# Two cross-attention layers on one core: the second layer's value products regrouped, VectorE's order written out beside them, sums of weights taken later

## The chip, the core and the metric

The kernel runs on one core of a Trainium2 chip. The core has a matrix engine (TensorE, PE in the profile, with its weight loads as PEld), a vector engine (VectorE, DVE), a scalar engine (ScalarE, ACT), a general engine (GpSimd, POOL), a sync engine that issues transfers (SyncE, SP) and 16 DMA engines. The metric is the device time of one execution in microseconds (us); lower is better. All arithmetic is in 32-bit floats.

## What is computed

For 8 batches, two layers one after the other. `x` holds 100 rows of 1024 for a batch, the context `ctx` 1444 rows of 512. Cut to what matters:

```
# layer 0
Q, K, V = x @ Wq + bq,  ctx @ Wk + bk,  ctx @ Wv + bv
x  = x + softmax(Q K^T / 32, over the context) V @ Wo + bo
# layer 1
q, k, v = x @ Wq + bq,  ctx @ Wk + bk,  ctx @ Wv + bv
w  = softmax(q k^T / 32, over the 100 QUERIES)
x  = layernorm(w v + x) * gamma + beta
```

In layer 1 the softmax runs over the queries, so the weights of one query do not add up to 1: their sum, times `bv`, has to be added to that query's row. That is why "sums of weights" appear below.

## The kernel before

The products of weight matrices are made first, so that the context is only multiplied by small matrices: scores are `(x Wq Wk^T) ctx^T`, and values are `(w ctx) Wv`. Large products use a scheme of seven half products in place of eight (`seven_products`, L172): each operand is cut in four, sums of the quarters are formed, and seven products go into banks of PSUM, which VectorE then adds to the result.

Layer 1 goes through the batches in a loop of blocks (L864). One block (`alternated`, L805) interleaves on TensorE 48 steps `A` (batch b's weights times its context rows, L513) with 44 steps `s` (scores of batch b+2, L542). When the scores of b+2 are complete, ScalarE copies them out (L554), VectorE transposes them in 16 instructions (L589), finds maxima (L656), ScalarE takes exponentials (L658), VectorE inverts the sums and multiplies (L661, L662), and GpSimd adds up the weights over the context (`weight_sums`, L675 to L680). Batches 6 and 7 have no batch b+2 ahead of them, so their blocks hold `A` steps alone. In the block of batch 5 two `s` steps go with each `A` step (`doubled`), so that batch 7's scores are early.

The values are the second part: `A` times `Wv` (512 by 1024). They are made in three sets: batches 0 to 4 by seven half products after block 5 (`project1_halves`, moving operands of 250 columns), batches 5 and 6 by 8 plain products after block 6 (`project1`, 200 columns), and batch 7 at the very end (`project_last`, L784). VectorE adds each result to `xT`, which holds the transposed queries (L612, L722).

A batch whose values are in is finished (`finish`, L770) by: 8 transposes on TensorE (L741), then on VectorE two additions of the bias times the sums of weights (L745), statistics (L751, L756, L758) and a scaling (L760); GpSimd takes the inverse root (L759), ScalarE scales (L762), GpSimd adds beta (L763) and issues the store (L764). Batch 7, the last, has its scaling and beta on VectorE in two halves (L767), each with its store (L768), the first from SP, the second from ACT. The table `finished` (L862) says at which step of which block a batch's transposes begin: batches 0, 1, 2 in block 6, batches 3 and 4 around `project1`, batches 5 and 6 in block 7. `weight_totals` (L682) turns the sums of weights of two batches by TensorE; it comes at step 8 of blocks 1, 3, 5 and 7.

TensorE's instructions stay in the order in which they are written. The other engines are ordered by a scheduler, which also chooses buffers. PSUM has two pools: six banks for scores, value products and transposes, two for `A` and for one pair of the seven products.

## Time and profile before

| | us |
|---|---|
| median of 4 runs (lowest, highest) | 642.47 (641.96, 642.88) |
| the profiled execution | 643.34 |
| its span on the core | 641.6 |
| TensorE busy | 631.2 (98%) |
| VectorE busy | 449.8 (70%) |
| ScalarE busy, GpSimd busy | 132.2, 101.7 |

The span is cut into lines by engine, and "busy" counts the time in which at least one instruction runs. Because matmuls are pipelined, the busy time of TensorE says that it never stands without work, not that it works at its peak; how long a matmul really holds the engine is read from the distance between the starts of two neighbours. A 32-bit product is recorded as two passes, so one `matmul` of the code is two records; a transpose is one. Layer 1's blocks fill the last 200 us of the span.

### The profile page before, as it was taken

The page shows a single profiled execution, that of the slowest core. Times are in us where ns is not written, and L with a number is a line of the kernel's source. Part 1 is how long each engine was busy: PE and PEld are TensorE (multiplying, and loading weights), DVE is VectorE, ACT ScalarE, POOL GpSimd, SP SyncE. Part 2 cuts the span into 40 slices and gives each one's busy share as a digit, 9 for nine tenths or more (in the row PEclk, how much of TensorE's full clock was granted, in tenths as well). Part 3 has the DMA queues.
Part 4 walks back from the last instruction along what each step waited for, and adds up shares of the span by engine and source line. Part 5 has one row for each costly group of instructions (what it writes and reads, how often), then busy time and mean ns, then how long its engine had stood idle before and what let it go on. Part 6 is the DMA issues. An engine that isn't in the chain of part 4 may idle for free.

```text
span 641.6 us, 9823 instructions
## 1 busy us (share of the span) xinstructions
PE 631.2 (98%) x3920; PEld 517.9 (81%) x3920; DVE 449.8 (70%) x848; ACT 132.2 (21%) x337; POOL 101.7 (16%) x121
## 2 busy tenths in 40 slices
PE   8999999999999999999999999999999999999994
PEld 7886445568885999999998655556999999999992
DVE  4999959669723775666655698238777655896994
ACT  1010010100103333212330000123433244330221
POOL 5000000009200000000010000007211222112773
PEclk9999999999999999999999999999999999999998
DMA  9928018000079799988996303046789999940122
GB/s 293 379 91 329 0 51 337 0 1 0 2 280 359 257 321 303 318 305 313 312 335 219 108 1 131 1 170 209 280 296 313 305 318 311 310 172 1 52 78 77
DMA packets 47961, 127.28 MB, mean 198 GB/s; under 512 B 3944, under 2 KB 6504, under 8 KB 47916
## 3 DMA queue, kind: packets, MB, share of 16 engines
q1 hardware_dynamic: 45454, 119.63, 53.8%
q0 software_dynamic: 2064, 6.56, 3.2%
q8 instruction: 31, 0.51, 0.3%
q10 hardware_dynamic: 398, 0.47, 0.2%
q14 instruction: 14, 0.11, 0.1%
HBM read 123.36 MB, written 3.28 MB: 197 GB/s over the span
## 4 chain that ended last, share of the span: by engine, by line
PE 81%; DVE 5%; issue 5%; POOL 5%; ACT 2%; DMA 1%; POOLq 0%; SPq 0%; DVEq 0%; ACTq 0%
PE s L542 23%; PE A L513 20%; PE qk_x L141 5%; PE g_x L141 5%; PE qk_y L141 4%; PE g_y L141 3%; PE vo_x L141 3%; DVE w L589 3%; PE o_x L141 3%; POOL z L763 2%; PE qk_w L141 2%; PE vo_y L141 2%; PE o_y L141 2%; PE g_w L141 2%; PE g_z L141 2%
## 5 line engine op out<-in xcount | busy, mean ns | idle before, releaser
L513 PE MATMUL A<-w,c 120*128 120x100 f32 (+1 forms) x1536 | 245.9, 265 | 0.0
L513 PEld LDWEIGHTS A<-w,c 120*128 120x128 f32 (+1 forms) x1536 | 215.5, 190 | 0.8
L589 DVE STREAM_TRANSPOSE w<-prob 32x384 f32<-32x384 f32 (+1 forms) x256 | 143.7, 561 | 46.3 <-ACT prob L554 15.8
L542 PE MATMUL s<-cT,g0T 128*100 128x131 f32 (+2 forms) x592 | 122.7, 296 | 0.0
L542 PE MATMUL s<-cT,g1T 128*100 128x131 f32 (+2 forms) x592 | 119.3, 296 | 0.0
L542 PEld LDWEIGHTS s<-cT,g0T 128*100 128x100 f32 x592 | 78.3, 167 | 8.3
L542 PEld LDWEIGHTS s<-cT,g1T 128*100 128x100 f32 x592 | 77.5, 167 | 8.9 <-ACT g1T L418 0.9
L554 ACT ACTIVATE prob<-s,c 100x393 f32<-100x393 f32 (+2 forms) x64 | 35.1, 559 | 116.9 <-PE s L542 116.6
L658 ACT ACTIVATE w<-w,negmax 120x100 f32<-120x100 f32 (+1 forms) x96 | 34.8, 364 | 75.1 <-DVE negmax L656 75.1
L469 POOL TENSOR_SCALAR xT<-xT,L_xattn_bo 128x800 f32<-128x800 f32 x8 | 20.8, 2607 | 134.0 <-PE qk_x L141 134.0
L571 DVE TENSOR_REDUCE maxima<-prob 100x1 f32<-100x394 f32 (+3 forms) x32 | 16.6, 528 | 28.1 <-ACT prob L554 27.9
L141 PE MATMUL qk_x<-qk 128*128 128x256 f32 x128 | 29.6, 389 | 0.9 <-DMA qk<-in_L_xattn_WkT 0.9
L141 PEld LDWEIGHTS qk_x<-qk 128*128 128x128 f32 x128 | 24.5, 196 | 5.2 <-DMA qk<-in_L_xattn_WqT 1.3
L850 POOL DMA_DIRECT2D vectors<-in_L_xattn_gamma x1 | 0.6, 602 | 163.2 <-DMA c<-in_ctx 163.2
L675 POOL TENSOR_TENSOR part<-w 120x500 f32<-120x500 f32 x8 | 10.0, 1250 | 103.5 <-PE s L542 47.3
L302 DVE SCALAR_TENSOR_TENSOR qk_L_xattn_bk<-qk,L_xattn_bk,qk_L_xattn_bk 128x1024 f32<-128x1024 f32 x14 | 17.9, 1277 | 3.9 <-DMA qk<-in_L_xattn_WqT 3.9
L612 DVE TENSOR_TENSOR xT<-xT,o_x 128x400 f32<-128x400 f32 (+1 forms) x24 | 13.5, 601 | 7.9 <-PE o_x L141 7.8
L418 ACT ACTIVATE g1T<-g_x,k 128x400 f32<-128x400 f32 x6 | 3.6, 594 | 74.2 <-PE g_x L141 63.8
L658 ACT ACTIVATION_READ_ACCUMULATOR w<-w,negmax 120x1 f32 (+1 forms) x96 | 17.9, 187 | 0.0
L763 POOL TENSOR_TENSOR z<-z,vectors 100x1024 f32<-100x1024 f32 x7 | 16.5, 2356 | 8.3 <-ACT z L762 8.3
L762 ACT ACTIVATE z<-z,rstd 100x1024 f32<-100x1024 f32 x7 | 8.0, 1149 | 39.7 <-POOL rstd L759 39.6
L662 DVE TENSOR_TENSOR w<-w,rtotal 120x400 f32<-120x400 f32 (+1 forms) x24 | 15.2, 634 | 0.5
(216 smaller groups left out, 872.1 us busy)
## 6 DMA issues: line engine op xcount, KB each, us to landing
cT<-in_ctxT SPq DMA_DIRECT2D x64, 722.0 KB, 6.7
c<-in_ctx SPq DMA_DIRECT2D x48, 768.0 KB, 7.4
c<-in_ctx SPq DMA_DIRECT2D x16, 512.0 KB, 6.5
vo<-in_L_xattn_Wo SPq DMA_DIRECT2D x8, 512.0 KB, 7.0
qk<-in_L_xattn_WqT SPq DMA_DIRECT2D x8, 512.0 KB
qk<-in_L_xattn_WqT SPq DMA_DIRECT2D x15, 256.0 KB, 5.3
qk<-in_L_xattn_WkT SPq DMA_DIRECT2D x15, 256.0 KB, 6.8
c<-in_ctx SPq DMA_DIRECT2D x16, 224.0 KB, 5.8
```

Of the source, the lines that this page charges most:

```text
L141: nc.tensor.matmul(banks[n // per][:, n % per * width : (n % per + 1) * width], lhs[i][:, n * P : (n + 1) * P], rhs[i], start=(fresh and i ...
L302: nc.vector.scalar_tensor_tensor(acc, src, cols[v][:, h : h + 1], acc, ALU.mult, ALU.add)
L469: nc.gpsimd.tensor_scalar(xT[:, e, :], xT[:, e, :], out_bias[:, e : e + 1], None, ALU.add)
L513: nc.tensor.matmul(ps[:, k * T : (k + 1) * T], c[m // CQ][:r, m % CQ, k * P : (k + 1) * P], w[:r, m, :], start=(m == 0 and k == 0), stop=( ...
L542: nc.tensor.matmul(banks[n // per][:T, cuts[n] - o : cuts[n + 1] - o], q[:, k, t0 : t0 + T], cT[k][:, cuts[n] : cuts[n + 1]], start=(k == ...
L554: nc.scalar.activation(p[:, part], ps[:T, : part.stop - part.start], AF.Identity, bias=key_bias[layer][:T, b : b + 1], scale=SCALE,)
L571: nc.vector.tensor_reduce(maxima[:, n : n + 1], p[:, part], AX.X, ALU.max)
L589: nc.vector.transpose(blocks(w, r, m0 * T + q * QD, T, MC - m0), blocks(p, q, m0 * MR + r * QD, MR, MC - m0),)
L612: nc.vector.tensor_tensor(to, to, ps[:, : n * width].rearrange("p (n t) -> p n t", n=n), ALU.add)
L658: nc.scalar.activation(w[:r, m0 + m, :], w[:r, m0 + m, :], AF.Exp, bias=negmax[:r, m : m + 1], accum_out=total[:r, m : m + 1])
L662: nc.vector.tensor_tensor(w[:r, grp, :], w[:r, grp, :], rtotal[:r].unsqueeze(2).to_broadcast([r, GM, T]), ALU.mult)
L763: nc.gpsimd.tensor_tensor(z, z, beta[:T], ALU.add)
```

## The change

The sets of batches become 0 to 3, 4 to 6, and 7. Both of the first two are made by seven half products, of 200 and 150 moving columns, after block 3 and after block 6; the plain products are gone. All sums of right operands are formed ahead of the products, in a buffer of their own. Two `s` steps per `A` step in block 5 are gone. The batches' finishing is spread over blocks 4, 5 and 7.

While a value product runs, VectorE keeps the order of the program (`Vector.in_order`), and the order is written by hand: the softmax of batch 5 (none of whose VectorE steps is taken before) and of batch 7 (of which 17 steps are taken) is drawn out step by step between the additions (`room`). In all softmaxes of layer 1 the three groups' maxima now come ahead of the three groups' inversions. The addition of the fourth half product goes ahead of the next one's in all seven-product stages that only add. The sums of weights are turned at step 27 in place of 8 (still 8 in block 7). The last batch's two stores change queues. The core of the diff:

```diff
+SETS = (range(0, 4), range(4, 7), range(7, 8))
+LATER = {(1, 5): 0, (1, 7): 17}
...
+                ins = getattr(nc.vector, op)(*args, **kw)
+                return tc.keep_in_program_order(ins) if self.in_order else ins
...
         W = pair("w", bank2)
         product(W, A22, T_[3], True)
+        if put is add:
+            add(1, 0, W)
         yield
...
-        softmax(s, parts)
+        s["softmax"] = softmax(s, parts)
+        for _ in islice(s["softmax"], LATER.get((layer, b))):
+            pass
...
-    def project1_halves(A, S, At):
-        n = G1 * T // 2
...
-        T_ = ([t1[:, i * n : (i + 1) * n] for i in range(2)], Bs[0], Bs[2], Bs[1])
...
-    def project1(b0, n, A, between):
-        for e in range(EC):
-            ps = bank(f"o1_{b0}_{e}")
-            for k in range(LC):
-                nc.tensor.matmul(...)
+    def project1(bs, A, S, At, between, room):
+        n, t0 = len(bs) * T // 2, bs[0] * T
...
+        T_ = [[sums[:, (2 * k + i) * n : (2 * k + i + 1) * n] for i in range(2)] for k in range(4)]
...
+        vector.in_order = True
+        right_sums(Bs, T_)
+        for _, steps in zip_longest(seven_products(f"o1_{t0}", A, Bs, S, T_, 4, n, add, add), room, fillvalue=0):
+            for _ in range(steps):
+                next(between)
+        run(between)
+        vector.in_order = False
...
-        for half, queue in ((slice(0, E // 2), nc.sync), (slice(E // 2, E), nc.scalar)):
+        for half, queue in ((slice(0, E // 2), nc.scalar), (slice(E // 2, E), nc.sync)):
...
-            for _ in range(2 if doubled else 1):
-                next(ahead, None)
+            next(ahead, None)
...
-    finished = {(B - 2, 0): 0, (B - 2, 14): 1, (B - 2, 28): 2, (B - 1, 6): G1, (B - 1, 22): G1 + 1}
+    finished = {(4, 2): 0, (4, 16): 1, (4, 30): 2, (5, 30): 3, (7, 2): 4, (7, 15): 5, (7, 28): 6}
...
+                if b % 2 and n == (8 if b == B - 1 else 27):
+                    weight_totals(batches[b - 1 : b + 1])
...
+            between, room = {3: (batches[5], (0, 3, 3, 3, 3)), 6: (batches[7], (1, 0, 1, 1))}[b]
+            project1(bs, *AS, t, between["softmax"], room)
```

## The prediction

> **What bounds the kernel now.** I read the busy table first, then TensorE's waits, then TensorE's timeline of the last 100 us, then VectorE and GpSimd beside it. From the page: the busy table, and the shares of the chain that ended last.

> ```profile
> PE 631.2 (98%) x3920; PEld 517.9 (81%) x3920; DVE 449.8 (70%) x848; ACT 132.2 (21%) x337; POOL 101.7 (16%) x121
> ...
> PE 81%; DVE 5%; issue 5%; POOL 5%; ACT 2%; DMA 1%; POOLq 0%; SPq 0%; DVEq 0%; ACTq 0%
> ```

> TensorE is busy for all of the span but its first 2 and last 8 us. Busy alone could hide waits, so its list of waits comes next (total, times, longest, in us):

> ```profile
> PE warm L90 <- DVE mhalf L105: 1.1, 1, 1.1
> PE qk_x L141 <- DMA qk<-in_L_xattn_WkT: 0.9, 1, 0.9
> PE qk_y L141 <- DVE qk_s L152: 0.2, 1, 0.2
> ```

> Three waits, all at the start. So in layer 1 the time is the length of TensorE's queue, plus the tail behind its last product. The change can win in two ways only, a shorter queue or a shorter tail, and it loses where an engine comes too late for TensorE. TensorE's timeline of the value stage (start, length, line, operation, count; a length runs to the modelled end of the last pass, so I use distances of starts):

> ```profile
> 563.85 3.56 PE L141 MATMUL o_x<-A1T,wv 128*128 128x250 f32 x16
> ...
> 587.49 0.36 PE L513 MATMUL A<-w,c 120*128 120x100 f32 x2
> ...
> 597.64 2.82 PE L513 MATMUL A<-w,c 120*128 120x100 f32 x24
> 600.29 1.04 PE L741 MATMUL z<-ident,xT 128*100 128x128 f32 x8
> 601.36 5.68 PE L718 MATMUL o<-A1T,wv 128*128 128x200 f32 x32
> 606.87 1.04 PE L741 MATMUL z<-ident,xT 128*100 128x128 f32 x8
> 607.75 5.58 PE L718 MATMUL o<-A1T,wv 128*128 128x200 f32 x32
> 613.16 1.70 PE L513 MATMUL A<-w,c 120*128 120x100 f32 x14
> ```

> The seven half products run without a gap from 563.85 to 587.49, 23.64 us for 112 passes: 0.2111 us a pass of 250 columns. The plain ones take 5.41 us for 32 passes from 607.75: 0.1691 us a pass of 200 columns, the same 0.84 ns a column. [...]

> **TensorE's queue, part by part.**
> 1. Value products. Before: 23.64 + 5.51 + 5.41 = 34.56 us. After: 112 passes of 200 columns, 112 x 0.1691 = 18.94, and 112 of 150 columns. No row has 150 columns with full weights. The bounds are the `A` pass, 0.1104, and the 200-column pass, 0.1691; 150 x 0.00084 = 0.127 lies above what weights need, so I take 0.1271: 14.23. Together 33.17: **-1.39** (-3.3 to +3.3 by the bounds).
> 2. Block 5. An `A` with two `s` repeats every 0.651 us (543.73 to 544.38 in the timeline), an `A` with one `s` every 0.4255 (33 pairs from 528.36 to 542.40), an `A` alone takes 0.2208. Before: 22 x 0.651 + 26 x 0.2208 = 20.06. After: 44 x 0.4255 + 4 x 0.2208 = 19.60. **-0.46.**
> 3. Transposes for finishing. 64 in both, the last 8 at the same place. Between `A` steps one adds 0.31 - 0.2208 = 0.089 us; two groups of 8 stood alone (1.07 and 0.88 us; the first holds a wait of 0.2 for `A1T`, which goes with the plain products). Before: 40 x 0.089 + 1.95 = 5.51. After, 32 stand behind an `s` and ahead of an `A`, which no row shows: from 0.089 (between `A`) to 0.134 (the slow group). I take 0.110, from the group without a wait: 32 x 0.110 + 24 x 0.089 = 5.66. **+0.15** (-0.5 to +0.9).

> The turned sums of weights are as many as before; moving them from step 8 to 27 costs TensorE nothing, since `wsum` is older there. The queue's sum is **-1.70 us**.

> **Does another engine come late?** I walked the changed kernel's order on each engine with these durations: additions to `xT` 0.57 us at 400 elements and 0.67 at 500 (so 0.45 at 300), sums of right operands 0.41 at 250 (0.35 at 200, 0.30 at 150), 0.585 a transpose, 0.56 a maximum, 0.57 to 0.66 a softmax product.
> - First set, t = 0 at its first product. Batch 3's copy lands at 0.8, the eight sums end at 3.5. The first two additions end at 4.6, three transposes at 6.3, the next additions at 7.4 and 9.3, three transposes at 11.1, the additions that free the first pair's banks for its last use at 12.2. TensorE wants those banks at 5 x 2.71 = 13.5: 1.3 us of cover, if all adds take 0.57. The remaining steps end at about 24; batch 5's weights are due after block 4, at 41.
> - Second set: the 16 transposes of batch 7 fill block 6 (10.6 us against 9.4); sums end at 3.1, the same banks are free near 9.2 and wanted at 10.2: 1 us of cover. Batch 7's weights are done at 10, due at 14.2.
> - Transfers: blocks 4 and 5 become longer or equal, and the pause between blocks 3 and 4 lets loads run ahead. The change adds no wait for a transfer.
> - The layer 0 stages and the other softmaxes only swap neighbours on VectorE; nearest wait there is zero, and I take zero.

> Where this cover is gone, the wait is the overrun itself, up to about 1 us a set.

> **The tail** is where the change gives back. Block 7 now finishes three batches (steps 2, 15, 28) instead of two (6, 22). VectorE's and GpSimd's timelines show what happens when they crowd:

> ```profile
> 592.13 1.27 DVE L760 SCALAR_TENSOR_TENSOR z<-z,mv,vectors 100x1024 f32<-100x1024 f32 x1
> ...
> 606.23 3.35 DVE L760 SCALAR_TENSOR_TENSOR z<-z,mv,vectors 100x1024 f32<-100x1024 f32 x1
> ...
> 624.05 1.78 DVE L760 SCALAR_TENSOR_TENSOR z<-z,mv,vectors 100x1024 f32<-100x1024 f32 x1
> ```

> ```profile
> 606.14 2.36 POOL L763 TENSOR_TENSOR z<-z,vectors 100x1024 f32<-100x1024 f32 x1 [1.26 <-ACT z L762]
> ...
> 622.39 2.35 POOL L763 TENSOR_TENSOR z<-z,vectors 100x1024 f32<-100x1024 f32 x1 [1.26 <-ACT z L762]
> ...
> 634.85 1.52 POOL L759 TENSOR_TENSOR rstd<-rstd,mhalf 100x1 f32<-100x1 f32 x1 [4.09 <-DVE rstd L758]
> ```

> L760 alone takes 1.27 us. At 606.23 it starts under a running L763 and ends at 609.58, 1.08 after L763 does: it stood still until L763 was over. Now the walk, t = 0 at the last batch's product (626.35 before). Batch 6's transposes begin 5.1 us ahead of the last 8, 1.2 later than before (6.3). Each finish costs VectorE about 4.5 us, and starts come 3.6 us apart, so batch 5's L760 ends near -1.2, its L763 runs from 0.9 to 3.3; batch 6's L760, due at 1.3, stands until 3.3 and ends at 4.5; then L759 0.6, L762 1.15, and batch 6's L763 from 6.3 to 8.7. The last batch's L760 is due at 634.68 - 626.35 = 8.3 and stands until 8.7: **+0.35** (0, if batch 6 runs 0.4 earlier, to +2.4, a whole L763).

> [...]

> **The stores.** The first half is issued from SP at 637.19 (0.31 long), its packets run from 637.97 to 639.39; the second from ACT at 637.86 (0.57), packets from 639.01 to 640.20. SP needs 0.78 us from issue to first packet, ACT 1.15. With the queues swapped the later half comes from SP: **-0.2** (0 to -0.37; both halves then share the DMA engines).

> **Sum:** -1.70 + 0.35 - 0.2 = **-1.55 us**. On the profiled execution's 643.34 that is 641.8; the median of the runs is 642.47, 0.87 below it, so I forecast 640.9.

> **Rivals.**
> - The fixed order holds TensorE: the cover of 1.3 and 1 us in the two sets is my estimate, from additions extrapolated to new widths. For it: VectorE has about 21.5 us of work beside 18.9 us of products in the first set. Against: only two products reuse banks. Overrun 0.5 us a set: 640.9 + 1.0 = 641.9.
> - The tail takes a whole L763, +2.4 instead of +0.35, since batch 6 slips by half a microsecond or more: 643.0. Against: GpSimd stood idle for 4.09 us ahead of the last L759 before.
> - Slower: the collisions chain. L763 of batch 4 ends only 0.4 us ahead of batch 5's L760; past that, L760 of batch 5 stands too (2.08 us, as at 606.23), everything behind it slips, and the last batch pays L763 (2.36) and the store's issue (0.6) on top: tail +3 to +3.5 against -1.9 elsewhere, 643.6 to 644.1, decided once batch 6's L763 ends later than 10.2 us after the last product's start. I put it at 643.9.
> - It does not do what it says: if a 150-column pass took over 0.152 us, all gain would be gone (645.5 at 0.1691). The 131-column `s` passes, near 0.114, speak against it.

> **Numbers.** Forecast (640.2 to 641.2) 0.60; fixed order 0.15; one whole collision 0.14; chain or slow passes 0.11. The smallest change that a measurement of this kernel tells from none is about 0.2%, 1.3 us: below 641.2 is faster, above 643.75 slower. So faster 0.60, same 0.29, slower 0.11. The range runs from 640.1 (no tail cost, stores at -0.37) to 643.0 (the whole collision).

> **What would show it.** Right: `o` passes of 0.169 and 0.127 us; no wait of TensorE in layer 1; block 5 near 19.6 us plus 8 transposes; L763 of batch 6 touching the last L760; the last store from SP. Wrong: gaps in the two value stages, or more than 15.5 us from the last product's start to the span's end (15.2 now).

## The result, and the profile after

The change made the kernel slower by 0.75 us: median 643.01 of 42 runs against 642.26 of 60 runs of the kernel before, ratio 1.0011 (95% interval 1.0007 to 1.0016). The forecast was 640.9. The profiled execution took 643.13, its span is 641.4. That this is no more than before's 643.34 misleads: before's profiled execution began 0.83 us late by chance. Its first `qk_y` product starts at 20.86 us, in the changed kernel at 20.03, and nothing ahead of it was changed. So from here on I measure from that product: to the first product of the last batch (`ol`), and from there to the span's end, which the traces give to 0.01 us (641.57 before, 641.36 after).

| from the profiled executions, us | before | after | predicted |
|---|---|---|---|
| `qk_y` to `ol` | 605.49 | 605.88 (+0.39) | -1.70 |
| `ol` to the span's end | 15.22 | 15.44 (+0.23) | +0.15 |

The sum of +0.39 and +0.23, +0.62 us, agrees with the medians (0.75, interval 0.45 to 1.03). The busy table and the chain's shares of the changed kernel:

```profile
PE 629.4 (98%) x3968; PEld 518.0 (81%) x3968; DVE 456.5 (71%) x864; ACT 131.9 (21%) x337; POOL 101.5 (16%) x121
...
PE 86%; DVE 6%; POOL 2%; issue 2%; ACT 2%; DMA 1%; POOLq 0%; DVEq 0%; SPq 0%; ACTq 0%
```

TensorE is busy 1.8 us less than before (631.2), and the time is longer all the same: the queue did become shorter, and TensorE now waits. Its list of waits (total, times, longest) has two lines that before had not:

```profile
PE o_y L156 <- DVE o_t L93: 1.1, 1, 1.1
...
PE z L759 <- DVE r L715: 0.5, 1, 0.5
```

**Wait 1, in the second set.** The timeline of all engines around it (start, length, engine, line, operation; idle time ahead and what ended it in brackets). L93 is the line of a helper through which much of VectorE's work goes: tell its operations by tile.

```profile
586.28 9.45 DVE L93 STREAM_TRANSPOSE w<-prob 32x384 f32<-32x384 f32 x16
...
595.76 1.52 DVE L93 TENSOR_REDUCE negmax<-w 120x4 f32<-120x400 f32 x3
...
596.43 0.38 ACT L682 ACTIVATE w<-w,negmax 120x100 f32<-120x100 f32 x1 [7.84 <-DVE negmax L93]
...
598.47 2.20 PE L156 MATMUL o_z<-A1T,wv 128*128 128x150 f32 x16
...
600.42 0.36 ACT L682 ACTIVATE w<-w,negmax 124x100 f32<-124x100 f32 x1
...
600.78 0.47 ACT L542 COPY A1T<-A 128x400 f32<-128x400 f32 x1
601.28 0.54 DVE L93 TENSOR_TENSOR o_t<-A1T 128x150 f32<-128x150 f32 x2 [4.00 <-ACT A1T L542]
...
601.74 2.28 PE L156 MATMUL o_y<-o_t,wv_s 128*128 128x150 f32 x16 [1.06 <-DVE o_t L93]
```

Read it from below. `o_y` waits for the first sum `o_t`; VectorE stood idle for 4.00 us ahead of that sum and was released by the copy L542 of batch 6's weighted features; and this copy, whose source was complete when TensorE went on to `o_x` at 596.41, started at 600.78, because in ScalarE's queue batch 7's twelve exponentials stand ahead of it, one every 0.36 us. The exponentials are late since VectorE's 16 transposes for them fill all of block 6. By starts the wait costs more than the 1.06 us of the list, which counts from a modelled end: `o_y` starts 3.27 us after `o_z` and the next product 2.12 after `o_y`, where the pace is 2.04, 1.3 us in all.

**Wait 2, in block 5.** The same view of an earlier stretch:

```profile
576.21 0.38 PE L713 MATMUL wsum_ps<-ident,wsum 124*100 124x124 f32 x2
...
577.88 0.18 DVE L93 RECIPROCAL rtotal<-total 120x4 f32<-120x4 f32 x1 [0.73 <-ACT w L682]
...
579.33 0.18 DVE L93 RECIPROCAL rtotal<-total 120x4 f32<-120x4 f32 x1 [0.66 <-ACT w L682]
...
579.54 0.58 DVE L93 TENSOR_TENSOR w<-w,rtotal 120x400 f32<-120x400 f32 x1
...
580.04 0.41 DVE L715 TENSOR_REDUCE r<-wsum_ps 100x2 f32<-100x248 f32 x1
...
580.50 0.32 PE L759 MATMUL z<-ident,xT 128*100 128x128 f32 x1 [0.49 <-DVE r L715]
```

The sums of weights of batches 4 and 5, now turned at step 27, hold a bank of PSUM (the memory that products are written to) from 576.21 until VectorE has read them (L715). VectorE comes to that only behind two of batch 6's softmax products, which wait for exponentials, and the transposes of batch 3's finish want the bank. VectorE stood idle for 0.73 and 0.66 us meanwhile: what held the sums was its order, not its load. By starts this wait costs 0.72 us: the transpose comes 0.66 late, the next one 0.06 more.

**The tail**, GpSimd and VectorE (L781 is GpSimd's addition of beta, L778 the scaling, L782 a store's issue, L777 the inverse root):

```profile
626.86 2.34 POOL L781 TENSOR_TENSOR z<-z,vectors 100x1024 f32<-100x1024 f32 x1 [1.84 <-ACT z L780]
...
627.15 3.13 DVE L778 SCALAR_TENSOR_TENSOR z<-z,mv,vectors 100x1024 f32<-100x1024 f32 x1
...
631.97 2.35 POOL L781 TENSOR_TENSOR z<-z,vectors 100x1024 f32<-100x1024 f32 x1 [1.26 <-ACT z L780]
...
634.24 1.27 DVE L778 SCALAR_TENSOR_TENSOR z<-z,mv,vectors 100x1024 f32<-100x1024 f32 x1
```

Batch 6's scaling stood under a running addition for 3.13 us, as foreseen; the last batch's did not (1.27). It starts 8.33 us after `ol`, the same as before, and VectorE's last instruction ends 11.47 after it (before 11.48). The 0.23 us are lost behind that, in the stores.

### The profile page after: what moved, and what is told of

It is laid out like the page before. It is cut to its first block, busy times and chain, and to the rows that moved or that the text cites. A ratio compares the mean times of both kernels' runs of the same rounds, so it can differ in the third digit from the quotient of the medians.

```text
span 641.4 us, 9939 instructions
## 1 busy us (share of the span) xinstructions
PE 629.4 (98%) x3968; PEld 518.0 (81%) x3968; DVE 456.5 (71%) x864; ACT 131.9 (21%) x337; POOL 101.5 (16%) x121
## 4 chain that ended last, share of the span: by engine, by line
PE 86%; DVE 6%; POOL 2%; issue 2%; ACT 2%; DMA 1%; POOLq 0%; DVEq 0%; SPq 0%; ACTq 0%
PE s L560 23%; PE A L531 20%; PE qk_x L156 6%; PE g_x L156 5%; PE qk_y L156 4%; PE o_x L156 4%; PE g_y L156 3%; PE vo_x L156 3%; DVE w L93 3%; PE o_y L156 3%; PE qk_w L156 2%; PE vo_y L156 2%; PE qk_z L156 2%; PE g_w L156 2%; PE g_z L156 2%
## 5 line engine op out<-in xcount | busy, mean ns | idle before, releaser
L93 DVE STREAM_TRANSPOSE w<-prob 32x384 f32<-32x384 f32 (+1 forms) x256 | 143.7, 561 | 37.3 <-ACT prob L572 15.1
L560 PE MATMUL s<-cT,g1T 128*100 128x131 f32 (+2 forms) x592 | 122.9, 297 | 0.0
L93 DVE TENSOR_TENSOR xT<-xT,o_x 128x400 f32<-128x400 f32 (+1 forms) x32 | 15.9, 540 | 3.5 <-PE o_x L156 3.2
L781 POOL TENSOR_TENSOR z<-z,vectors 100x1024 f32<-100x1024 f32 x7 | 16.5, 2354 | 8.1 <-ACT z L780 8.1
L759 PE MATMUL z<-ident,xT 128*100 128x128 f32 x64 | 16.4, 274 | 0.5 <-DVE r L715 0.5
L93 DVE TENSOR_TENSOR w<-w,rtotal 120x400 f32<-120x400 f32 (+1 forms) x24 | 15.6, 650 | 0.7
```

The source lines that it names most:

```text
L93: ins = getattr(nc.vector, op)(*args, **kw)
L560: nc.tensor.matmul(banks[n // per][:T, cuts[n] - o : cuts[n + 1] - o], q[:, k, t0 : t0 + T], cT[k][:, cuts[n] : cuts[n + 1]], start=(k == ...
L759: nc.tensor.transpose(ps[:T, e * P : (e + 1) * P], xT[:, 4 * j + e, b * T : (b + 1) * T], ident)
L781: nc.gpsimd.tensor_tensor(z, z, beta[:T], ALU.add)
```

## The experiments

Theory: the regrouping did shorten the queue by about 1.7 us, and two waits, one in each of block 5 and the second set, and the stores took it back. Rivals: VectorE's fixed order holds TensorE, so that another wait comes up wherever one is removed; or the regrouping brings nothing. The table has all kernels; ratios are to the kernel before, run on the same chip beside each group of kernels (its median there was 642.05 to 642.51, so medians of different groups are compared with care). Kernels with the same code behind `ol` differ by up to 0.11 us in the last column, which is its scatter.

| kernel | median (runs) | ratio, 95% | `qk_y` to `ol` | `ol` to end |
|---|---|---|---|---|
| before | 642.26 (60) | | 605.49 | 15.22 |
| after | 643.01 (42) | 1.0011 (1.0007-1.0016) | 605.88 | 15.44 |
| e1 sums of weights early | 644.46 (7) | 1.0032 (1.0020-1.0043) | 607.88 | 15.49 |
| e2 copy on VectorE | 641.82 (11) | 0.9993 (0.9984-1.0002) | 604.58 | 15.46 |
| e3 stores back | 642.81 (11) | 1.0006 (0.9998-1.0015) | 605.89 | 15.42 |
| e4 the three together | 640.98 (11) | 0.9980 (0.9971-0.9989) | 603.86 | 15.41 |
| e5 e4, free order | 640.78 (8) | 0.9976 (0.9966-0.9986) | 603.86 | 15.43 |
| e6 exponentials later | 641.36 (11) | 0.9984 (0.9975-0.9993) | 604.58 | 15.45 |
| e7 copy three times | 644.21 (10) | 1.0027 (1.0017-1.0037) | 608.61 | 15.44 |
| e8 e4, finishes earlier | 640.73 (11) | 0.9975 (0.9966-0.9983) | 603.86 | 15.37 |
| e9 before, stores swapped | 642.20 (11) | 1.0003 (0.9994-1.0011) | 605.49 | 15.24 |
| e10 copy twice | 643.53 (11) | 1.0016 (1.0007-1.0025) | 606.44 | 15.47 |
| e11 copy five times | 646.42 (5) | 1.0061 (1.0048-1.0075) | 609.54 | 15.38 |
| e12 e5, tail in halves | 640.79 (11) | 0.9979 (0.9971-0.9988) | 603.86 | 15.35 |
| e13 e4 without batch 6's store | 640.64 (11) | 0.9978 (0.9969-0.9987) | 603.86 | 15.18 |
| e14 e4, finishes on VectorE | 640.75 (11) | 0.9979 (0.9970-0.9987) | 603.86 | 15.27 |

### The two waits

**e1** turns the sums of weights of batches 4 and 5 at step 8 again (those of blocks 1 and 3 too, on which no wait hung), which is to take wait 2 away.

```diff
-                if b % 2 and n == (8 if b == B - 1 else 27):
+                if b % 2 and n == 8:
```

> The changed kernel, but the sums of weights of batches 4 and 5 are turned and summed at step 8 of block 5, as before, instead of step 27. Theory (two new waits of TensorE and the stores eat the gain of the queue): the wait of the z transposes for r in block 5 goes, TensorE's queue is 0.5 to 0.66 us shorter from block 4 to the last product, time 643.0 - 0.6 = 642.4. Rival (VectorE is simply too full around block 5, and some other bank is late as well): the wait returns at another instruction, 643.0.

Measured 644.46, 1.45 us slower than the changed kernel; neither theory nor rival foresaw that. The wait for `r` went, and the second set starts 0.73 us earlier (575.65 us after `qk_y` instead of 576.38). But the copy that `o_y` waits for hangs on VectorE and ScalarE, not on TensorE, and came not earlier but 0.33 us later; the wait of `o_y` grew to 2.11 us. And then something new. The value products' timeline, and the busy time by stretch (stretch, its length, busy time and count of each engine; the number after POOL's brackets is TensorE's granted clock):

```profile
597.35 2.20 PE L156 MATMUL o_z<-A1T,wv 128*128 128x150 f32 x16
601.67 3.56 PE L156 MATMUL o_y<-o_t,wv_s 128*128 128x150 f32 x16 [2.11 <-DVE o_t L93]
605.03 2.64 PE L156 MATMUL o_x<-o_t,wv_s 128*128 128x150 f32 x16
607.50 2.21 PE L156 MATMUL o_w<-o_t,wv 128*128 128x150 f32 x16
```

```profile
602.00:603.00 1.00, 1.00 (x8) 1.00 (x7) 1.00 (x5) 0.00 (x0) 0.00 (x0) 0.74 0.00 0
603.00:604.00 1.00, 1.00 (x5) 1.00 (x5) 0.97 (x5) 0.00 (x0) 0.00 (x0) 0.50 0.00 0
...
605.00:606.00 1.00, 1.00 (x6) 1.00 (x6) 1.00 (x4) 0.00 (x0) 0.00 (x0) 0.55 0.00 0
606.00:607.00 1.00, 1.00 (x10) 1.00 (x10) 0.72 (x3) 0.00 (x0) 0.00 (x0) 1.00 0.00 0
```

`o_y`'s 16 passes take 3.36 us from start to next start instead of 2.04: behind the wait the clock stood at 0.50, five passes in a microsecond instead of ten. From `o_y` to `ol` it is 25.84 us here and 24.17 in the changed kernel: 1.67 us lost to the clock, which no theory had.

**e2** lets VectorE make batch 6's copy, which is to take wait 1 away.

```diff
-                    if name.startswith("A1"):
+                    if name.startswith("A1") and name != "A1_6":
                         nc.scalar.copy(dst, src)
                     else:
                         nc.vector.tensor_copy(dst, src)
```

> The changed kernel, but batch 6's weighted features (A1T) are copied from the bank by VectorE, behind batch 7's maxima, instead of by ScalarE behind batch 7's twelve exponentials. Theory: the first sums of right operands of the second set start near 598 instead of 601.3, the 1.06 us wait of o_y goes, the queue is 1.2 us shorter, time 643.0 - 1.2 = 641.8. Rival (the fixed order of VectorE is what holds TensorE, the copy is only the first to show it): a wait of 0.5 us or more comes up at a later product of that set, time 642.5 or more.

Measured 641.82, queue 1.30 us shorter. VectorE's and TensorE's rows, with the copy on VectorE:

```profile
597.50 0.56 DVE L544 COPY A1T<-A 128x400 f32<-128x400 f32 x1
...
598.17 0.54 DVE L93 TENSOR_TENSOR o_t<-A1T 128x150 f32<-128x150 f32 x2
...
600.80 2.21 PE L156 MATMUL o_y<-o_t,wv_s 128*128 128x150 f32 x16
```

The sum starts at 598.17, 2.6 us ahead of `o_y`, which follows `o_z` (598.76) at the products' own pace of 2.04 us. No other wait comes up in the set. This speaks for the theory and against the fixed order as the cause.

**e6** removes the same wait by another way: batch 7's maxima and exponentials move behind the copy in ScalarE's queue, the copy stays where it was.

```diff
-LATER = {(1, 5): 0, (1, 7): 17}
+LATER = {(1, 5): 0, (1, 7): 16}
...
-            between, room = {3: (batches[5], (0, 3, 3, 3, 3)), 6: (batches[7], (1, 0, 1, 1))}[b]
+            between, room = {3: (batches[5], (0, 3, 3, 3, 3)), 6: (batches[7], (1, 1, 0, 1, 1))}[b]
```

> The changed kernel, but batch 7's maxima and exponentials are issued inside the second set, behind batch 6's copy in ScalarE's queue, instead of ahead of it; the copy stays on ScalarE. Theory (the queue order of ScalarE made the wait of 1.06 us): the first sum starts by 598, no wait of o_y for o_t, the queue 1.2 us shorter, time 641.8 as with the copy on VectorE. Rival (the second set has too little room for batch 7's softmax): a wait of 0.5 us or more at a later product of the set or at block 7's first product, 642.3 or more.

Measured 641.36 and a queue of 604.58 us, to the hundredth that of e2. The copy runs at 596.39, the first sum at 596.92, and the exponentials between 600 and 605 are early enough. So what counted was the order in ScalarE's queue, not the engine of the copy.

**e4** puts the three edits together.

> The three edits together: sums of weights at step 8, batch 6's copy by VectorE, the stores' queues of before. Theory (the three causes are apart and add): 643.0 - 0.6 - 1.2 - 0.27 = 640.9, some 1.4 us less than the kernel before, no wait of TensorE in layer 1. Rival (fixed order or regrouping brings nothing): 642 or more, with waits of TensorE in the value stages.

Measured 640.98, 1.4 us below before (642.35 on the same chip). Its list of waits has only the one at the very start:

```profile
PE warm L105 <- DVE mhalf L120: 1.1, 1, 1.1
```

Its queue is 603.86 us: 0.72 less than e2's, so with wait 1 out of the way wait 2 is worth 0.72; 2.02 less than after's, and 1.63 less than before's. The regrouping does bring what it was said to.

**e5** leaves VectorE's order in the value stages to the scheduler, on top of e4.

```diff
-        vector.in_order = True
+        vector.in_order = False
         right_sums(Bs, T_)
```

> The kernel with the three edits, but VectorE's order in the two value stages is left to the scheduler. Theory (the fixed order neither costs nor gains much, since after the three edits TensorE waits for nothing): 641.0 within 0.3, no wait of TensorE over 0.2 us in the value stages. Rival (the fixed order itself is a burden, as the prediction's first rival had it): 640.5 or less. Second rival (without it the sums and additions that free banks come late): a wait of 0.3 to 1 us in a value stage, 641.3 to 642.

Measured 640.78 with e4's queue to the hundredth and no wait in layer 1. The fixed order neither costs nor gains here; the rival falls. A free order with the two waits still in was not run; there the trace speaks against VectorE's order as the cause of wait 1, since VectorE stood idle for 4.00 us ahead of the sum.

### The clock behind a wait

The stop of 2.11 us in e1 and the low clock behind it came with another edit, so three kernels lengthen the wait alone: the changed kernel with batch 6's copy made two, three or five times (same values).

```diff
-                        nc.scalar.copy(dst, src)
+                        for _ in range(3 if name == "A1_6" else 1):
+                            nc.scalar.copy(dst, src)
```

> The changed kernel, but ScalarE makes batch 6's copy three times over (the same values, 0.47 us each), so that the sums start 0.94 us later and TensorE's wait at o_y grows from 1.06 to 2.0 us; nothing else is changed. Theory (a standstill of about 2 us of TensorE lowers the clock that is granted, as in the run with early sums of weights, where the clock stood at 0.50 for 3.4 us behind a wait of 2.11 us): 643.0 + 0.94 + 1.6 = 645.5 in most executions, clock near 0.5 for about 3 us behind the wait. Rival (the slow passes there came with the early sums of weights, not with the wait): 643.0 + 0.94 = 643.95, clock 1.0 behind the wait.

> The changed kernel with batch 6's copy made twice: TensorE's wait at o_y grows from 1.06 to about 1.55 us. Theory (a wait lowers the clock for about 3 us in a share of executions that grows with its length: none seen at 1.06, about half at 2.0): fewer than half of the executions 1.2 to 1.7 us above the rest; median 643.0 + 0.47 = 643.5. Rival (about 2 us is a sharp limit): all near 643.5.

> The changed kernel with batch 6's copy made five times: the wait grows to about 2.95 us. Theory (the share of executions with the lowered clock grows with the wait): nearly all executions pay it, 643.0 + 1.88 + 1.5 = 646.4. Rival (the share does not depend on the length): half of them at 644.9 and half at 646.4.

| wait of `o_y`, from the list | kernel | runs |
|---|---|---|
| 1.1 | after | median 643.01, clock 1.00 behind the wait |
| 1.6 | e10 | 11 of 11 from 643.05 to 644.00 |
| 2.1 | e7 | 5 from 643.43 to 643.98, 5 from 644.44 to 645.46 |
| 2.1 | e1 | 2 at 643.43 and 643.78, 5 from 644.35 to 645.34 |
| 3.1 | e11 | 1 at 645.35, 4 from 646.06 to 646.84 |

The same stretch of the profile in e10 and in e7, columns as above. e10:

```profile
604.00:605.00 1.00, 1.00 (x10) 1.00 (x9) 0.96 (x4) 0.00 (x0) 0.00 (x0) 1.00 0.06 16
```

e7:

```profile
604.00:605.00 1.00, 1.00 (x6) 1.00 (x5) 0.97 (x4) 0.00 (x0) 0.00 (x0) 0.50 0.08 16
```

In the profiled executions the queue is longer than the wait explains by 1.68 us in e7 and in e11 (`ol` later by 2.73 and 3.66, of which the later `o_y` is 1.05 and 1.98), and by nothing in e10 (0.56 and 0.56). So the drop came with the wait alone, and by the times in none of 11 executions at 1.6 us, in 10 of 17 at 2.1 (9 without the doubtful one below), and in 4 of 5 at 3.1. The shares are read from the times; the granted clock of each run, averaged over its span, fits them: 0.995 to 0.998 in all runs of the changed kernel and of e10 and in the lower groups, 0.992 to 0.995 in the upper ones (the run of e7 at 644.44, with 0.995, could belong to either, and is the doubtful one). "Most executions" for e7 was too much; that the share does not depend on the length is unlikely, though five runs of e11 are few.

How long the clock stays low is read from its mean in each microsecond: it falls at 602.48 us in e1, 603.24 in e7 and 604.56 in e11, and is back at 605.90, 606.66 and 607.96. That is 3.4 us in each, behind waits of 2.11, 2.12 and 3.15 us, and it begins 0.81, 1.15 and 1.14 us after the products resume (601.67, 602.09 and 603.42). In e10, with a wait of 1.60 us, the clock stays at 1.00 from 599 to 608.

Why only a part of the executions pays, no run here shows: an execution of e1, e7 or e11 without the drop was not profiled. One thing that differs between two profiled executions is when the clock changes: in before it rises to 1.00 at 6.40 us from the span's start, in the changed kernel at 4.19, and it stays there for 631.47 us in both.

### The tail

**e3** and **e9** test the swap of the stores' queues alone, in the changed kernel and in the kernel before (shown for e3; e9's edit is the reverse).

```diff
-        for half, queue in ((slice(0, E // 2), nc.scalar), (slice(E // 2, E), nc.sync)):
+        for half, queue in ((slice(0, E // 2), nc.sync), (slice(E // 2, E), nc.scalar)):
```

> The changed kernel, but the two halves of the last store come from the queues of before (first SP, then ACT). Theory (the swap costs 0.27): from the last product's start to the span's end 15.2 us instead of 15.5, time 642.75. Rival (the prediction's figure, SP starts packets sooner than ACT): 15.7 us and 643.2.

> The kernel before with one edit: the halves of the last store come from ScalarE's queue first and SP's second, as in the changed kernel. Theory (the queue does not matter, the place does: first store 0.8 us to its first packet, second 1.15, whichever queue; the longer tail of the changed kernel comes from something else): from the last product's start to the span's end 15.25 us as before, time 642.3. Rival (the swap is what made the tail 0.16 to 0.24 us longer): 15.45 us, time 642.5. Second rival (the prediction's term): 15.05 us, 642.1.

The tail changes by -0.02 us in e3 and by +0.02 in e9, that is, the swap is worth nothing in either direction; theory and rival of e3 are both wrong, the theory of e9 is right (e3's median, 642.81, lies 0.2 below the changed kernel's, within the scatter of the runs). From issue to first packet the first store takes 0.78 us from SP (before, e3) and 0.82 and 0.81 from ACT (after, e9); the second takes 1.15 and 1.13 from ACT (before, e3), 1.17 and 1.19 from SP (after, e9). The delay goes with the place, not with the queue.

What differs is the stretch that the packets of each half take, from the first one's start to the last one's end (from the traces' packets). First half and second half take 1.43 and 1.19 us before and 1.42 and 1.18 in e9, but 1.50 and 1.44 after, 1.65 and 1.44 in e3, 1.63 and 1.42 in e4. In the latter three, batch 6's store ends less than 0.1 us ahead of the first packet; before it ended 4.9 us ahead (633.05 and 637.97).

**e8** was to move batch 6's store away by earlier finishes, on top of e4.

```diff
-    finished = {(4, 2): 0, (4, 16): 1, (4, 30): 2, (5, 30): 3, (7, 2): 4, (7, 15): 5, (7, 28): 6}
+    finished = {(4, 2): 0, (4, 16): 1, (4, 30): 2, (5, 30): 3, (7, 2): 4, (7, 12): 5, (7, 22): 6}
```

> The kernel with the three edits, but in block 7 the finishes of batches 4, 5 and 6 start at steps 2, 12 and 22 instead of 2, 15 and 28, so that batch 6's L763 and store are over about 1.5 us earlier. Theory (the 0.16 us by which the tail is longer than before comes from batch 6's store, whose packets end just as the last store's start): from the last product's start to the span's end 15.25 instead of 15.41, time 640.8. Rival (the finishes, now nearer to each other, collide with GpSimd's additions and reach the last product): 0.3 us or more longer, 641.3 or more.

Inconclusive: the first packet of batch 6's store comes 9.88 us after `ol` instead of 9.87. Batch 5's L778 was held to 1.91 us by batch 4's L781, and its scaling on ScalarE stands behind the copy of batch 7's `A` in either kernel, so its L781 again holds batch 6's L778 (3.15). Tail and time are e4's within the scatter.

**e13** leaves batch 6's store out of e4, **e14** makes it earlier by taking batches 5 and 6 off GpSimd.

```diff
-            nc.gpsimd.dma_start(out=out[b], in_=z)
+            if b != B - 2:
+                nc.gpsimd.dma_start(out=out[b], in_=z)
```

> The kernel with the three edits, but batch 6's output is not written (the store is left out; everything else is computed). Theory (the packets of batch 6's store, which end less than 0.1 us ahead of the last store's first packet, make that store's packets slower): first half's packets take 1.43 us and the second half's 1.18, as in the kernel before, instead of 1.63 and 1.42, and the tail from the last product's start to the span's end is 15.2 instead of 15.4. Rival (the stretch has another cause, or is chance): 1.4 us for the second half and a tail of 15.4.

```diff
+        if b == B - 2 or b == B - 3:
+            nc.vector.scalar_tensor_tensor(z, z, rstd, beta[:T], ALU.mult, ALU.add)
+            nc.gpsimd.dma_start(out=out[b], in_=z)
+            return
```

> The kernel with the three edits, but batches 5 and 6 are scaled and shifted in one VectorE instruction, as the last batch is, instead of by ScalarE and then by GpSimd's L781. Theory (batch 6's L778 no longer stands under a running L781, and its store is over some 3 us before the last one): L778 of batch 6 1.3 instead of 3.13 us, tail 15.2, time 640.8, the least of the kernels here but within their scatter. Rival (VectorE, not GpSimd, is then what is late: the last product's sums stand behind batch 6's instructions): tail 15.6 or more, 641.2.

e13: packets 1.40 and 1.19 us, tail 15.18, 0.23 less than e4's. e14: batch 6's store ends 3.0 us ahead (632.39, first packet 635.41), packets 1.40 and 1.19, and batch 6's scaling is not held any more:

```profile
626.12 1.28 DVE L778 SCALAR_TENSOR_TENSOR z<-z,mv,vectors 100x1024 f32<-100x1024 f32 x1
```

Its tail is 15.27, 0.14 less than e4's and not 0.23, since the last batch's sums now stand behind batch 6's second scaling: the last L778 starts 8.42 after `ol` instead of 8.32. So the packets of the last two stores take about 0.24 us longer (from first to last 2.44 us in e4, 2.20 in e13 and in e14) when the store ahead of them ends right in front of them. A single packet takes no longer (on average 107 ns in the first half before and 105 after, 114 in e4's and 115 in e13's); they start later. Why packets that are over still delay the next ones, no run here shows.

**e12** tries to use VectorE's 0.46 us of idleness ahead of the last two instructions.

```diff
-        nc.vector.scalar_tensor_tensor(z, z, mv[:, 0:1], gamma[:T], ALU.subtract, ALU.mult)
+        for h in (slice(0, E // 2), slice(E // 2, E)) if b == B - 1 else (slice(0, E),):
+            nc.vector.scalar_tensor_tensor(z[:, h], z[:, h], mv[:, 0:1], gamma[:T, h], ALU.subtract, ALU.mult)
...
-            nc.gpsimd.dma_start(out=out[b], in_=z)
+            (nc.scalar if b == B - 2 else nc.gpsimd).dma_start(out=out[b], in_=z)
```

> The kernel with the three edits and VectorE's order left free, and two edits in the tail: batch 6's output is issued from ScalarE instead of GpSimd, so that GpSimd's L777 (rstd of the last batch) does not stand behind that issue, and the last batch's L778 is made in two halves, so that L777 can run between them. Theory (VectorE's 0.46 us of idleness ahead of the last two instructions is the wait for L777): most of 0.3 us goes, tail 15.1 instead of 15.4, time 640.6. Rival (L777 is held until both halves are done, whatever stands ahead of it): tail 15.4 to 15.5, time 640.9.

The idle time went: the last two instructions start 9.64 us after `ol` instead of 10.05 (e4). But the tail is 15.35, against 15.43 in e5, its basis. The last stores now run into batch 6's packets (these end 0.58 us after the first half's first packet, and the first half takes 2.01 us), and most of the 0.41 us is given back there, in line with e13.

## Why the prediction was wrong

**TensorE's queue: right.** The first set takes 18.98 us (523.04 to 542.02; predicted 18.94). A pass of 150 columns takes 2.04 / 16 = 0.1275 us (0.1271), so the second set without its wait 14.28 (14.23). The forecast's 14.23 leaned also on a least time that the weights of a pass need; no run shows one, only 0.1275 us for the 150-column pass and 0.1104 for an `A` pass (2.65/24, from 597.64 to 600.29 before). Block 5 without its transposes, its turned sums and its wait comes to about 19.7 (19.60). Transposes between `s` and `A` add 0.107 to 0.110 (0.110). The sum, where nothing waits, is -1.63 in e4 against -1.70.

**"Moving them from step 8 to 27 costs TensorE nothing, since `wsum` is older there": failed, 0.72 us** (e2 to e4). The step looked at what the turned sums wait for and not at what waits for them: a PSUM bank that VectorE gives back only in its own order, now in the middle of a softmax.

**"Second set: ... sums end at 3.1, ... 1 us of cover": failed, 1.30 us** (after to e2). The sums began 4.87 us after the set's first product (601.28 - 596.41). I had walked VectorE's order and taken the copy ahead of it as done at 0.8, without walking ScalarE's queue, where twelve exponentials of 0.36 us stand in front; it was done at 4.84. The transposes that "fill block 6" were right (9.45 us), and what followed from them on ScalarE was left out. **The first set's** cover of 1.3 us held, with 1.8 us in the trace (banks free at 534.81, wanted at 536.60); there nothing stood ahead of the copy, and it was done at 0.7 (0.8).

**The tail.** The collision of +0.35 cost nothing: batch 6's L781 ended at 8.41 instead of 8.7, and the last L778, due at 8.33, ran unhindered. That was my stated lower bound. **The stores' -0.2 failed**: the two delays from issue to first packet that I gave to SP and ACT belong to the first and the second store, whichever queue (e9: +0.02 from the swap). In their place came a cost that the prediction did not have, about +0.23, from batch 6's store that now ends right in front of the last one (e13).

**The sum** becomes -1.63 + 1.30 + 0.72 = +0.39 for the queue and +0.23 for the tail. Of the rivals, the first had the right sign of trouble (a gap in a value stage) with the wrong cause: in e5, without the two waits, the fixed order is harmless. The second rival's figure, 643.0, is the measured time, but by luck: its cause, a whole L763 in the last batch's way, did not come about.

Two figures of the prediction do not follow from its own terms, and nothing turns on either. Without a tail cost and with the stores at -0.37 its sum gives 640.4, not 640.1, as the lower end; and a gain of 1.55 us over 112 passes is used up at 0.141 us a pass, not at 0.152.

The waits also hide each other: wait 2 alone, taken away, made wait 1 longer by more than it saved (1.05 us against 0.73), and the longer wait then cost 1.67 us of clock (e1). Only in e2 and e4 do the pieces add.

## What to carry to other kernels

When a step is moved, walk the queue of every engine that stands between producer and consumer, the one that makes a plain copy included, and ask what holds the copy, not only how long it takes; and for whatever is written into PSUM, ask when the reader gives the bank back. Try fixes for two waits on the same engine together as well as one by one: removing the first alone can make the second longer. Count more for a wait of TensorE than its length: behind one of 2.11 us in e1 the clock stood at 0.50, and 1.67 us were lost on top.
